# A fifth room between scores and weighting, warming steps and a new written-out order in a pre-norm attention and expert kernel

## Chip, core and metric

One core of one Trainium2 chip runs the whole kernel. The metric is the device time of one execution in microseconds (us); the kernel before has a median of 277.43 us over three runs (276.83 to 277.89).

## What is computed

The input is `x`, four batches of 1024 tokens with 128 features. One layer is applied: attention, then a mixture of experts, each on a layer-normed input and each with a residual.

```python
x = x + attn(layernorm(x));  x = x + moe(layernorm(x))
# attn, 8 heads of 16
Q, K, V = silu(x@Wq), silu(x@Wk), silu(x@Wv);  U = x@Wu
s = (Q @ K.T + rel_bias[i - j + 255]) / 4      # set to NEG above the diagonal
w = silu(s)                                    # and for keys that are all zero
out = (w @ V) * silu(U)
# moe: top 2 of 8 gates, softmax over the two
y = sum_e gate[e] * ((x @ w_in[e].T) @ w_out[e].T)
```

The weights are `silu`, not a softmax, so that no row sum is needed. An expert has no nonlinearity between its two matrices; the kernel folds them into one matrix of 128 x 128 (`wfold`).

## The kernel before

**Groups.** The queries are worked on in groups of 512 (four tiles of 128), two per batch; the last group is split into two of 256, which makes nine. For a group, the keys are gone through in 73 units over the whole kernel. One unit fills four score banks of up to 512 columns: keys against queries for the four heads 2k + parity, k = 0 to 3.

**Score step (S, `attend`).** TensorE (PE) fills four PSUM banks with scores (L492). Near the diagonal VectorE (DVE) adds the bias from the table `near` and writes the sum to a room `w` in SBUF (L511), and ScalarE (ACT) applies silu in place (L514). Far from it the bias is one number for a head, and ACT goes from PSUM to `w` alone (L519). **Weighting step (W, `weigh`).** PE multiplies `w` with V and adds it up in one bank `av` (L470); after a group's last unit DVE gates the sum (L479). The rooms `w` come from the pool `wpool`, which has `WBUFS = 4` of them: a score step whose room is still unread has to wait for the weighting step four units back.

**The other steps.** P and Q prepare the first and the second half of a batch: norm, K, Q, V, U. The key mask takes a DVE comparison `nz` (L387), a small product, and `kmask` (L394). K makes the bias tables (`constants`) and clears the second of the two rooms for V (L257, GpSimd, POOL). G folds experts. C, D and E (`finish`) carry a group from attention to its gates; the norm's statistics and the gates take a round trip through DRAM on the SyncE (SP) queue. X, Y and Z apply the experts, a tile at a time: `experts` scales the input by each gate first and sums in PSUM (L96, L650); `experts_then_gates`, for the last two groups, takes the product with all experts first and gates afterwards, in a scratch tile `both` from `spool` (L672 to L685). The result leaves by `store` (L691).

**What sets the order.** Each engine executes its instructions in the order in which they are written. The string `ORDER` is that order: `load_all` comes first, and then each letter advances its lane to its next `yield`. PSUM has a ring of seven banks for everything but `av` (`RING`, handed out in turn by `misc()`); a step that asks for a bank waits until the instruction that reads the bank's last use is done. The 73 letters S are 0 to 4 ahead of the 73 letters W.

**The start.** `load_all` begins with `HEAT = 18` dummy products of 128 x 128 on PE (`ident` against itself, L96; each is four 32-row pieces and two passes). POOL clears the first room for V in one memset of 2048 columns (L169) and some small tiles. DVE widens the bias row, `rb` (L146), and only then normalizes the first block (L316, L321, L330, with POOL's power L325); PE transposes it (L337) and ACT copies it to `xnT` (L338).

Of the kernel before, what the change touches and what calls it, by code (L numbers as in the profile page):

```python
# [8 lines left out]
F32 = mybir.dt.float32  # L9
# [7 lines left out]
P = 128  # L17
H = 8
HD = 16
NQ = 4  # L20
# [3 lines left out]
SB = 512  # L24
TPB = SB // P
# [6 lines left out]
OFF = -3.0e38  # L32
EULER = 2.718281828459045
RING = 7
HEAT = 18
LAST = 2


# [2 lines left out]


ORDER = (
    "PPQPQKPPQKPKSPSPSQQSWWSWGSWQPWSQWSPSCSWQPSCCQKWGSPWPSWWSWPKQSWGSWSWSCWSWPSWPSGDSQQDPQWSCPP"
    "WWSWQWSQDWSSCESCDWPEPCSCWQWEDCSWPCSWCQDSWDCSWDDDCPGSPPWQCDSQWSWSGWESGWPSWSWSDEWECQEDPEDEEC"
    "GDQWWSXSWSQCXECSCEXSECQWSCEXPWPWSDEDQPCQWSDDWDSYDSWQEESWDCYCCYCDCSWWWESCYCSPCWCCSZDCQWSEDZ"
    "SDEWPEQQWSEZSDWWDQDCDQSDCDWZDSDCXCSEWEWEWCCESWEECXXEESQWDSEWDDXSEDEYCSEDDWWDSCCYDCCCSCDCDY"
    "CSCYCDWCDESDWWEDDSZDWWEDWDEYEEYEYYZECZEEECEYEECZXEYEXEEZCZZZXZXZ"
)


# [1 line left out]
def preln_silu_attention_moe(  # L53
# [14 lines left out]
    nc = tc.nc  # L68
    B, S, D = x.shape
    NR = rel_biasT.shape[1]  # L70
    NT = S // P
    NB = S // SB
    NC = HID // P
    WBUFS = 4

    cpool = ctx.enter_context(tc.tile_pool(name="cpool", bufs=1))
    xpool = ctx.enter_context(tc.tile_pool(name="xpool", bufs=B))
# [10 lines left out]
    def misc():  # L88

        return ps_s.tile([P, SB], F32, tag="bank", name="bank")  # L90

    def product(out, stationary, moving, start=True, stop=True):


        for q in range(0, P, 32):
            nc.tensor.matmul(  # L96
                out[q : q + 32, :], stationary[:, q : q + 32], moving, start=start, stop=stop
            )
# [13 lines left out]
    NPAD = MAXLEN - 1 + TAB  # L112
    FAR = TAB - MAXLEN

    rb = spool.tile([P, 8 * D], F32, tag="both", name="rb")[:H, :NPAD]
    wcat = cpool.tile([P, 4, D], F32, tag="wcat", name="wcat")
    wgT = cpool.tile([P, GW], F32, tag="wgT", name="wgT")
    stats_d = dpool.tile([2 * B * NB, 32, 4, 32], F32, tag="stats_d", name="stats_d")
# [8 lines left out]
    def load_near(par, to, src, pitch, n):  # L127
# [2 lines left out]
            bass.AP(src.tensor, src.offset, [[1, P], [2 * pitch, NQ], [1, n]]),  # L130
        )

    def load_all():

        pt = misc()
        for i in range(HEAT):
            product(pt[:, :P], ident, ident)

        load_x(0, 0)
        nc.scalar.dma_start(rb[:, NPAD - NR :], rel_biasT)  # L140
        load_w(1, wk)
        load_near(0, FAR, rel_biasT, NR, MAXLEN)

        nc.vector.memset(one, 1.0)
        nc.scalar.activation(one, one, AF.Silu)
        nc.vector.tensor_copy(  # L146
            rb[:, : NPAD - NR], rb[:, NPAD - NR : NPAD - NR + 1].to_broadcast([H, NPAD - NR])
        )
        nc.scalar.dma_start(ext[:, :], rb)
        load_w(0, wq)  # L150
        load_x(0, 1)
        load_near(1, FAR, rel_biasT[1:2, :], NR, MAXLEN)

        load_near(0, FAR - P, ext[0:1, FAR - P :], NPAD, P)
        load_near(1, FAR - P, ext[1:2, FAR - P :], NPAD, P)
        load_w(2, wv)
        load_w(3, wu)
        nc.gpsimd.memset(wgT, 0.0)

        nc.gpsimd.memset(ones8, 1.0)  # L160
        nc.gpsimd.affine_select(
            out=ones8, in_=ones8, compare_op=ALU.is_ge, fill=0.0,
            base=0, pattern=[[-HD, H]], channel_multiplier=1,
        )
        nc.gpsimd.affine_select(
            out=ones8, in_=ones8, compare_op=ALU.is_ge, fill=0.0,
            base=HD - 1, pattern=[[HD, H]], channel_multiplier=-1,
        )
        nc.gpsimd.memset(vps[0], 0.0)  # L169
        nc.gpsimd.memset(euler, EULER)  # L170
        for st in stats:
            nc.gpsimd.memset(st, 0.0)
        nc.scalar.dma_start(wgT[:, :E], w_gateT)

        for n in range(2, B * NB):
            load_x(n // NB, n % NB)
        for e0 in range(0, E, 2):

            if e0 % 4 == 0:
                room = gpool.tile([P, 2, 2, 2, NC, D], F32, tag="wide", name=f"w_in_out_{e0}")  # L180
            both = room[:, e0 // 2 % 2]
            for t, w in zip((both[:, 0], both[:, 1]), (w_in, w_outT)):
                nc.sync.dma_start(t, w[e0 : e0 + 2].rearrange("e (c p) d -> p e c d", p=P))
            experts_in.append(both)
# [18 lines left out]


    one = cpool.tile([P, 1], F32, tag="one", name="one")
    ident = cpool.tile([P, P], F32, tag="ident", name="ident")
    make_identity(nc, ident)
    mhalf = cpool.tile([P, TPB], F32, tag="mhalf", name="mhalf")
# [18 lines left out]
    def constants():  # L227


        pt = misc()  # L230
        nc.tensor.matmul(
            pt[:, :H], rb[:, :1].to_broadcast([H, P]), ident[:H, :H], start=True, stop=True
        )
        for par in range(2):
            nc.scalar.copy(
                near[:, par, :, : FAR - P],
                pt[:, :H].rearrange("p (k q) -> p q k", q=2)[:, par, :]
                .unsqueeze(2).to_broadcast([P, NQ, FAR - P]),
            )
        nc.vector.tensor_scalar(cscaled, pt[:, :H], SCALE, None, ALU.mult)  # L240
        yield

        for par in range(2):
            diag = near[:, par, :, TAB - P : TAB]
            nc.gpsimd.affine_select(
                out=diag, in_=diag, compare_op=ALU.is_ge, fill=NEG,
                base=P - 1, pattern=[[0, NQ], [-1, P]], channel_multiplier=-1,
            )
            nc.vector.tensor_copy(near[:, par, :, TAB:], diag)  # L249
            yield  # L250

        nc.gpsimd.iota(
            rank, pattern=[[0, TPB], [-1, E]], base=E, channel_multiplier=0,
            allow_small_or_imprecise_dtypes=True,
        )
        yield
        nc.gpsimd.memset(vps[1], 0.0)  # L257
        yield

    def fold():  # L260

        for e0, both in zip(range(0, E, 2), experts_in):
            for e in range(2):
                pt = misc()
                for c in range(NC):
                    product(
                        pt[:, :D], both[:, 0, e, c, :], both[:, 1, e, c, :],
                        start=(c == 0), stop=(c == NC - 1),
                    )
                nc.scalar.copy(wfold[:, e0 + e, :], pt[:, :D])  # L270
                yield
# [368 lines left out]
    def experts(b, t0, gated):  # L640

        y = xs[b][:, t0 : t0 + TPB, :]
        for i in range(TPB):
            pt = misc()
            for e in range(E):
                product(
                    pt[:, :D], gated[:, i, e, :], wfold[:, e, :],
                    start=(e == 0), stop=(e == E - 1),
                )
            nc.vector.tensor_tensor(y[:, i, :], pt[:, :D], y[:, i, :], ALU.add)  # L650
            if i == TPB - 1:
                store(b, t0, TPB, y)
            yield

    def experts_then_gates(b, t0, nt, x2T, gates):

        EH = SB // D
        y = xs[b][:, t0 : t0 + nt, :]
        for i in range(nt):

            both = spool.tile([P, 2 * EH, D], F32, tag="both", name="both")
            gy, other = both[:, : EH + 1, :], both[:, EH + 1 :, :]
            for e0 in (EH, 0):
                pt = misc()
                product(
                    pt, x2T[:, i, :], wfold[:, e0 : e0 + EH, :].rearrange("p e d -> p (e d)")
                )
                for e in range(EH):
                    ye = pt[:, e * D : (e + 1) * D]
                    gate = gates[:, i, e0 + e : e0 + e + 1]  # L670
                    if e0:
                        nc.scalar.activation(  # L672
                            other[:, e, :] if e < EH - 1 else gy[:, EH, :], ye, AF.Copy, scale=gate
                        )
                    else:
                        nc.vector.scalar_tensor_tensor(
                            gy[:, e, :], ye, gate,
                            other[:, e, :] if e < EH - 1 else y[:, i, :],
                            ALU.mult, ALU.add,
                        )  # L680
                yield
            half = EH // 2
            nc.vector.tensor_tensor(gy[:, :half, :], gy[:, :half, :], gy[:, half:EH, :], ALU.add)
            nc.vector.tensor_tensor(gy[:, 0, :], gy[:, 0, :], gy[:, EH, :], ALU.add)
            nc.vector.tensor_tensor(y[:, i, :], gy[:, 0, :], gy[:, 1, :], ALU.add)  # L685
            if i == nt - 1:
                store(b, t0, nt, y)
            yield

    def store(b, t0, nt, y):  # L690
        nc.sync.dma_start(  # L691
            out[b, t0 * P : (t0 + nt) * P, :].rearrange("(i p) d -> p i d", p=P), y[:, :nt, :]
        )
# [9 lines left out]
    lanes["P"] = [prepare(b, 0) for b in range(B)]  # L703
    lanes["Q"] = [prepare(b, 1) for b in range(B)]
    lanes["G"] = [fold()]
    lanes["K"] = [constants()]

    def step(lane):
# [52 lines left out]
```

## Time and profile before

| what | us |
|---|---|
| median of the runs (lowest, highest) | 277.43 (276.83, 277.89) |
| the profiled execution | 276.35 |
| its span, from first to last instruction | 274.6 |
| PE, from its first score step to the start of its last product | 13.2 to 270.1 |
| last arithmetic (DVE L685) ends | 271.8 |
| DVE busy, 0 to 110 us | 80.3 |
| DVE busy, 110 us to the end | 149.5 |
| mean cost of one `w` add on DVE, 512 columns (L511) | 0.68 |

The page gives busy time by engine, then the span in slices, the chain of work that ended last, and the costliest groups of instructions. PE's busy time is not a measure of its load: the ends of matmuls are modelled, so an engine that waits inside a row of matmuls can still be shown as busy. What PE loses is read from the starts of its matmuls: equal rows of matmuls have equal start-to-start times where nothing holds them.

### The profile page before, as it was taken

What the parts mean: (1) busy time and instruction counts of PE and PEld (TensorE: products, weight loads), DVE (VectorE), ACT (ScalarE), POOL (GpSimd) and SP (SyncE); (2) the same over time, 40 slices, a digit from 0 to 9 for tenths busy, and PEclk for the clock granted to TensorE, in tenths of its full rate; (3) what the DMA queues carried; (4) which work ended last, traced back from release to release, by engine and by line L of the source; (5) the groups of instructions that cost most, each with busy time, mean ns of one, the idle gap of its engine ahead of it and who ended that gap; (6) DMA issues with size and microseconds to landing.
All of it is one profiled execution on the core that took longest, in us unless ns stands there. A gap on an engine that the chain in (4) does not pass through costs nothing.

```text
span 274.6 us, 10777 instructions
## 1 busy us (share of the span) xinstructions
PE 264.8 (96%) x4694; PEld 145.2 (53%) x4694; DVE 229.8 (84%) x594; ACT 194.0 (71%) x316; POOL 88.6 (32%) x101
## 2 busy tenths in 40 slices
PE   7799999999999999999999999999998999999993
PEld 7344443344444234444465347565675776775872
DVE  5597656569976977999989898999899998898994
ACT  2568998879899898889768866575965467684030
POOL 7410136600544712372024241351360343111010
PEclk9999999999999999999999999999999999999999
DMA  5899930330004032272080483217022621845022
GB/s 176 214 301 287 290 128 5 117 117 2 0 5 124 35 77 84 81 300 91 5 309 2 123 333 97 79 41 284 31 82 97 256 80 43 308 143 211 5 60 60
DMA packets 33315, 34.88 MB, mean 127 GB/s; under 512 B 4068, under 2 KB 29676, under 8 KB 32372
## 3 DMA queue, kind: packets, MB, share of 16 engines
q1 hardware_dynamic: 32516, 33.89, 38.3%
q8 instruction: 37, 0.61, 0.9%
q10 hardware_dynamic: 752, 0.31, 0.4%
q14 instruction: 10, 0.08, 0.1%
HBM read 31.74 MB, written 2.45 MB: 124 GB/s over the span
## 4 chain that ended last, share of the span: by engine, by line
PE 85%; DVE 8%; POOL 2%; issue 2%; ACT 1%; POOLq 0%; DVEq 0%
PE bank L96 31%; PE bank L492 29%; PE av L470 22%; DVE w L511 3%; DVE gated L635 2%; PE bank L541 2%; POOL rstd L325 1%; PE bank L569 1%; POOL vp L169 1%; DVE den L608 1%; ACT w L519 1%; DVE attended L479 0%; ACT w L514 0%; POOL xn L330 0%; DVE near L249 0%
## 5 line engine op out<-in xcount | busy, mean ns | idle before, releaser
L511 DVE TENSOR_TENSOR w<-bank,near 128x512 f32<-128x512 f32 (+2 forms) x220 | 116.5, 589 | 18.0 <-PE bank L492 15.0
L514 ACT ACTIVATE w<-w 128x1024 f32<-128x1024 f32 (+2 forms) x110 | 98.2, 915 | 40.5 <-DVE w L511 37.8
L492 PE MATMUL bank<-qT,kT 32*128 32x512 f32 (+3 forms) x864 | 91.0, 483 | 1.4 <-DVE x L650 0.8
L519 ACT ACTIVATE w<-bank,cscaled 128x512 f32<-128x512 f32 (+3 forms) x136 | 70.2, 604 | 10.4 <-PE bank L492 5.9
L470 PE MATMUL av<-w,vp 128*32 128x512 f32 (+3 forms) x864 | 74.0, 454 | 0.4 <-DVE turned L276 0.3
L492 PEld LDWEIGHTS bank<-qT,kT 32*128 32x128 f32 x864 | 39.7, 184 | 39.5 <-DVE w L511 14.9
L96 PE MATMUL bank<-wfold,gated 128*32 128x128 f32 x1792 | 53.9, 273 | 0.3 <-issue 0.3
L96 PEld LDWEIGHTS bank<-wfold,gated 128*32 128x32 f32 x1792 | 48.3, 110 | 9.2 <-issue 4.6
L470 PEld LDWEIGHTS av<-w,vp 128*32 128x32 f32 x864 | 23.2, 109 | 34.6 <-issue 26.3
L635 DVE TENSOR_TENSOR gated<-gated,x2T 128x1024 f32<-128x1024 f32 x28 | 35.8, 1288 | 0.9 <-DMA gated<-gates_d 0.9
L289 POOL TENSOR_TENSOR stats<-rs,mhalf 128x4 f32<-128x4 f32 x13 | 13.2, 1019 | 46.8 <-DVE rs L288 44.0
L96 PE MATMUL bank<-xnT,wcat 128*32 128x512 f32 x192 | 24.3, 597 | 0.5 <-ACT xnT L338 0.4
L605 POOL TENSOR_TENSOR ex<-euler,d 128x4 f32<-128x4 f32 (+1 forms) x9 | 9.6, 1061 | 41.0 <-DVE d L603 37.0
L406 POOL TENSOR_TENSOR vp<-v,kmask 128x256 f32<-128x256 f32 x16 | 9.8, 632 | 31.8 <-ACT v L404 31.8
L305 POOL TENSOR_TENSOR mean<-attended,mean 128x512 f32<-128x512 f32 x7 | 9.3, 1324 | 19.8 <-DMA mean<-stats_d 19.8
L672 ACT ACTIVATE both<-bank,gates 128x128 f32<-128x128 f32 x16 | 4.5, 375 | 14.9 <-DVE gates L619 11.0
L305 POOL TENSOR_TENSOR mean<-xT,mean 128x512 f32<-128x512 f32 x6 | 7.7, 1283 | 20.4 <-DMA mean<-stats_d 20.4
L96 PEld LDWEIGHTS bank<-xnT,wcat 128*32 128x32 f32 x192 | 5.3, 109 | 13.3 <-issue 5.2
L371 ACT ACTIVATE kT<-bank,sel 128x512 f32<-128x512 f32 x16 | 11.0, 690 | 0.2 <-PE bank L96 0.2
L306 POOL TENSOR_TENSOR x2T<-mean,x2T 128x512 f32<-128x512 f32 x7 | 9.8, 1402 | 0.6
L284 DVE BATCH_NORM_STATS2 stats<-x 128x6 f32<-128x256 f32 x26 | 9.8, 418 | 0.1
L96 PEld LDWEIGHTS bank<-w_in_out 128*32 128x32 f32 x256 | 7.0, 110 | 4.5 <-DVE w L511 2.4
(87 smaller groups left out, 204.4 us busy)
## 6 DMA issues: line engine op xcount, KB each, us to landing
gated<-gates_d SPq DMA_DIRECT2D x7, 2048.0 KB, 8.2
mean<-stats_d SPq DMA_DIRECT2D x13, 256.0 KB, 3.6
x<-in_L_attn_x SPq DMA_DIRECT2D x8, 256.0 KB, 6.4
w_in_out<-in_L_ffn_w_in SPq DMA_DIRECT2D x4, 512.0 KB, 7.4
w_in_out<-in_L_ffn_w_out SPq DMA_DIRECT2D x4, 512.0 KB, 7.5
xT<-in_L_attn_x_T SPq DMA_DIRECT2D x8, 256.0 KB, 4.4
x2T<-stats_d SPq DMA_DIRECT2D x7, 256.0 KB, 3.7
out<-x SPq DMA_DIRECT2D x7, 256.0 KB, 2.3
```

Of the source, the lines that this page charges most:

```text
L96: nc.tensor.matmul(out[q : q + 32, :], stationary[:, q : q + 32], moving, start=start, stop=stop)
L284: nc.vector.bn_stats(st[:, 3 * i : 3 * i + 6], src[:, i : i + 2, :].rearrange("p i d -> p d i"))
L289: nc.gpsimd.tensor_tensor(st[:, TPB * 3 : TPB * 4], rs, mhalf, ALU.pow)
L305: nc.gpsimd.tensor_tensor(mean, srcT, mean, ALU.subtract)
L306: nc.gpsimd.tensor_tensor(dst, mean, dst, ALU.mult)
L371: nc.scalar.activation(kT[:, par, s0 : s0 + SB], pk, AF.Silu, scale=sel[:, par : par + 1])
L470: nc.tensor.matmul(acc[k * 32 : (k + 1) * 32, nt * P - n : nt * P], vp[:, j, par, k, :, :].rearrange("p q c -> p (q c)"), w[:, k, c : c + ...
L492: nc.tensor.matmul(ps[k][:, c : c + n], kT[k * 32 : (k + 1) * 32, par, j * P : (j + 1) * P], qT[k * 32 : (k + 1) * 32, lo : lo + n], start ...
L511: nc.vector.tensor_tensor(w[:, k, :nn], ps[k][:, :nn], near_of(k, parts), ALU.add)
L514: nc.scalar.activation(w[:, k : k + 2, :nn], w[:, k : k + 2, :nn], AF.Silu, scale=SCALE)
L519: nc.scalar.activation(w[:, k, lo:hi], ps[k][:, lo:hi], AF.Silu, bias=cscaled[:, h : h + 1], scale=SCALE,)
L635: nc.vector.tensor_tensor(wide_g[:, i], wide_g[:, i], x2T[:, i : i + 1, :].to_broadcast([P, E, P]), ALU.mult)
```

## The change

Seven edits, and no arithmetic of the result is changed.

- `WBUFS` goes from 4 to 5. The tile `both` of the last experts, and the start's `rb`, no longer have a room of their own in `spool`; they take their turn in the ring of rooms `w`.
- `HEAT` goes from 18 to 10, and the dummy products use a tile `heat` that DVE sets to 1, in place of POOL's `ident`.
- A lane H (`warm`) does two dummy products per step; the order has six H: three before the first score step, one in the middle, two at the very end.
- Each room for V is cleared in four memsets of 512 columns.
- `experts` stores two tiles at a time in place of four, `experts_then_gates` one in place of two.
- The order string is new. The same steps stand in it, with S up to 5 ahead of W. The first bias step K stands ahead of the first transpose, K's other steps are spread, and the four last X (experts of the third-last group) are mixed with the last Z so that the string ends in X, then HH. In the string before it ends in XZ.

```diff
-HEAT = 18
+HEAT = 10
-    "PPQPQKPPQKPKSPSPSQQSWWSWGSWQPWSQWSPSCSWQPSCCQKWGSPWPSWWSWPKQSWGSWSWSCWSWPSWPSGDSQQDPQWSCPP"
...
-    "CSCYCDWCDESDWWEDDSZDWWEDWDEYEEYEYYZECZEEECEYEECZXEYEXEEZCZZZXZXZ"
+    "PPQKHPHPQPQHPKSPSQQKPSWWSGSKWGSPKWQPWSQWSSWPSQPPSWWCSWPSWQSSCWSPPPQSQWSWSWWPSWPSQQWSWWSDGC"
...
+    "WEYCEDDDWSWESCWDCDCWDYCWDEWDDDZEEYYEYZEYEEEYEYEZECECECEZEZCZXZZXZXZXHH"
-    WBUFS = 4
+    WBUFS = 5
-    rb = spool.tile([P, 8 * D], F32, tag="both", name="rb")[:H, :NPAD]
+    rb = wpool.tile([P, NQ * SB], F32, tag="w", name="rb")[:H, :NPAD]
+    def clear(vp):
+        for i in range(0, NT, 2):
+            nc.gpsimd.memset(vp[:, i : i + 2], 0.0)
-            product(pt[:, :P], ident, ident)
+            product(pt[:, :P], heat, heat)
-        nc.gpsimd.memset(vps[0], 0.0)
+        clear(vps[0])
+    heat = cpool.tile([P, P], F32, tag="heat", name="heat")
+    nc.vector.memset(heat, 1.0)
-        nc.gpsimd.memset(vps[1], 0.0)
+        clear(vps[1])
+    def warm():
+        while True:
+            pt = misc()
+            for i in range(2):
+                product(pt[:, :P], heat, heat)
+            yield
-            if i == TPB - 1:
-                store(b, t0, TPB, y)
+            if i % 2:
+                store(b, t0 + i - 1, 2, y[:, i - 1 :])
-            both = spool.tile([P, 2 * EH, D], F32, tag="both", name="both")
-            gy, other = both[:, : EH + 1, :], both[:, EH + 1 :, :]
+            both = wpool.tile([P, NQ * TPB, D], F32, tag="w", name="both")
+            gy, other = both[:, : EH + 1, :], both[:, EH + 1 : 2 * EH, :]
-            if i == nt - 1:
-                store(b, t0, nt, y)
+            store(b, t0 + i, 1, y[:, i:])
+    lanes["H"] = [warm()]
```

More of the change, by code (lines that the diff above doesn't have):

```diff
@@ L34 @@
 RING = 7
-HEAT = 18
+HEAT = 10
 LAST = 2
 ORDER = (
-    "PPQPQKPPQKPKSPSPSQQSWWSWGSWQPWSQWSPSCSWQPSCCQKWGSPWPSWWSWPKQSWGSWSWSCWSWPSWPSGDSQQDPQWSCPP"
-    "WWSWQWSQDWSSCESCDWPEPCSCWQWEDCSWPCSWCQDSWDCSWDDDCPGSPPWQCDSQWSWSGWESGWPSWSWSDEWECQEDPEDEEC"
-    "GDQWWSXSWSQCXECSCEXSECQWSCEXPWPWSDEDQPCQWSDDWDSYDSWQEESWDCYCCYCDCSWWWESCYCSPCWCCSZDCQWSEDZ"
-    "SDEWPEQQWSEZSDWWDQDCDQSDCDWZDSDCXCSEWEWEWCCESWEECXXEESQWDSEWDDXSEDEYCSEDDWWDSCCYDCCCSCDCDY"
-    "CSCYCDWCDESDWWEDDSZDWWEDWDEYEEYEYYZECZEEECEYEECZXEYEXEEZCZZZXZXZ"
+    "PPQKHPHPQPQHPKSPSQQKPSWWSGSKWGSPKWQPWSQWSSWPSQPPSWWCSWPSWQSSCWSPPPQSQWSWSWWPSWPSQQWSWWSDGC"
+    "WSWQPPDSQDWSSCESWWSDWCGECQDSWPSWCHSWCCQDCESCDWDDSCDQGCDWECPPSWSCWWESWSGQWSGWSGEQQPSDWPWSWQ"
+    "DDEDECQWSQCCXSWECPSEXCESCWSQPCDDWQPSDEWXSXESWPDWEECSDCCCYWCCSCCYDSWDCSCWDYCSWEYSWCEZQSWSWE"
+    "DEQQZPEESPZWEWQDDSCDWDDSWDCZSDCDDWEDSXCEEQQECCSECWXEEXESEDDXWSWEDWECESYCCWDCSWCCSYDDCDSWSD"
+    "WEYCEDDDWSWESCWDCDCWDYCWDEWDDDZEEYYEYZEYEEEYEYEZECECECEZEZCZXZZXZXZXHH"
 )
```

## The prediction

> **What bounds the kernel now.** I read the busy times and the chain of the page first, then the waits, then the timeline at three places: the start, a hole in a score step, the end.
>
> ```profile
> PE 264.8 (96%) x4694; PEld 145.2 (53%) x4694; DVE 229.8 (84%) x594; ACT 194.0 (71%) x316; POOL 88.6 (32%) x101
> ...
> PE 85%; DVE 8%; POOL 2%; issue 2%; ACT 1%; POOLq 0%; DVEq 0%
> ```
>
> PE carries 85% of the chain. Its 96% says little, since ends are modelled, so I took from the trace the start-to-start times of PE's matmuls by row: a unit's four 512-column scores take 1.07 us undisturbed, their weighting 0.86, one expert tile (64 matmuls) 1.77. At these paces PE's work from the first score step (13.2 us) to 270.1 is 237.5 us. What rows took over their own kind's undisturbed pace (lower quartile, after equal predecessors, holes over 0.06 us) adds up to **14.3 us of waiting**: 9.05 in score steps, 2.82 in weighting steps, 2.4 elsewhere. The rest, 5, is the price of changing kinds of step, which the new order leaves alone (66 changes from scores to 32-column products against 66).
>
> ```profile
> PEld bank L492 <- DVE w L511: 14.9, 25, 0.8
> PEld bank L492 <- ACT w L519: 5.8, 11, 0.8
> PEld av L470 <- ACT w L514: 2.7, 6, 0.8
> ```
>
> The columns are us in total, times, longest. They are waits of the weight load, partly covered by matmuls still running, so their sum isn't PE's loss; but they name the releasers. Score steps wait for banks that DVE or ACT still reads, and weighting steps for silu. A hole as an example:
>
> ```profile
> 57.84 0.50 PE L492 MATMUL bank<-qT,kT 32*128 32x128 f32 x6
> 58.79 1.13 PE L492 MATMUL bank<-qT,kT 32*128 32x128 f32 x10 [0.45 <-ACT w L519]
> ```
>
> Six of sixteen score matmuls go, then the bank ring is full for nearly 1 us. DVE is the second bound: 80.3 of the first 110 us are busy, but 149.5 of the remaining 162 to its last result, 92%.
>
> **The fifth room and the order.** I summed every step's PE work at the paces above. In the old string a weighting step is written a median of 6.45 us of PE work after the end of its score step (tenth percentile 3.9, least 2.8); in the new 8.41 (4.8, 3.8). What must happen between is, for a unit near the diagonal, four adds (2.48 us, DVE L511) and the second silu (1.06, L514), 3.5 us, and whatever DVE has queued before. So the 2.82 us of weighting waits have 1 to 2 us more cover each, more than the longest release of 0.8 in the row above: I take 2.0 away (ends 0 and 2.82). Score waits are not about rooms: DVE and ACT still read the seven banks, and there are still seven. The room helps them only by letting PE do a weighting step, 0.86 us, in the meantime if the order puts one there. Bounds: all of 9.05 goes, or waits grow (the slower rival). A change of order that leaves DVE's work the same must lie near the bottom: I take 1.0. The middle gives **-3.0**. DVE's idle share after 110 us (12 us) leaves room for that. The adds need no room sooner than before: none of DVE's listed waits in L511 is for a weighting step, so rooms delay PE, not DVE.
>
> **The H in the middle** and its bank: 16 matmuls by 27.7 ns (an expert tile's 1.77 us over 64), **+0.44**; 0 if it falls in a hole, 0.44 if not. The pair HH at the end is 0.9 us of PE beside a store, which takes longer: 0.
>
> **The start.**
>
> ```profile
> 1.80 1.80 POOL L169 MEMSET vp<- 128x2048 f32 x1
> ...
> 2.48 1.58 DVE L146 COPY rb<-rb 8x256 f32<-8x256 f32 x1 [1.57 <-DMA rb<-in_L_attn_rel_bias]
> ...
> 3.99 0.74 DVE L316 BATCH_NORM_STATS2 st<-x 128x6 f32<-128x256 f32 x2
> ...
> 5.02 1.02 POOL L325 TENSOR_TENSOR rstd<-rs,mhalf 128x4 f32<-128x4 f32 x1 [1.10 <-DVE rs L321]
> ...
> 7.39 0.66 PE L337 MATMUL bank<-ident,xn 128*128 128x128 f32 x4
> ```
>
> A copy of 256 columns lasts 1.58 us because it finishes 0.45 us after POOL's memset, 3.61. [...] The transposes at 7.39 also wait for the old heating, which runs to 7.46; the xn they need was ready at 7.02. [...] The copy of `near` ahead of `nz` (DVE L249, 11.45 to 12.29) goes behind it, but `nz` started at 12.28 with the key at 12.24, so that alone gives 0.04, and the second copy (0.42) now stands among the adds. K's two ACT copies of `near` (0.54 each) come ahead of xnT on ACT, behind DMA issues that end about 5.9, so they end at 7.0, just in time. Sum: between -0.9 and +0.4, I take **-0.5**.
>
> [...] In this trace the dummy matmuls go every 53.4 ns until 5.3 us and every 27.3 afterwards, and the record of the granted clock begins at 5.27, 3.8 us after the first. [...]
>
> **The end.**
>
> ```profile
> 270.41 0.29 DVE L650 TENSOR_TENSOR x<-bank,x 128x128 f32<-128x128 f32 x1 [0.52 <-PE bank L96]
> 270.62 0.41 DVE L683 TENSOR_TENSOR both<-both 128x256 f32<-128x256 f32 x1
> ...
> 271.47 0.29 DVE L685 TENSOR_TENSOR x<-both 128x128 f32<-128x128 f32 x1
> ```
>
> After the last product (L650's bank) three more adds of the gated path stand ahead of the last store; PE's products are already over. In the new string the last Z is ahead of the last X, so the end is one add of 0.29: the last store is issued at 270.7 instead of 271.8, **-1.05**. Store to landing was 1.86 (271.79 to 273.65, 128 KB, with 256 KB more ahead of it); the new last one is 128 KB with 64 ahead: 0 to 0.3 less, taken as 0.
>
> **Stores.** 18 instead of 9, each some 0.39 us of SP (the last two issues). SP is in order and a store waits for its add, so loads of the norm's statistics behind it wait as well. Those loads wait for a later DVE transpose in any case, and the whole queue is some 90 issues by 0.4, 36 of 275 us: 0, up to +3.5 if all nine further issues were on the path. **The scratch tile in the ring**: a Y or Z step needs the room of five allocations before, whose weighting is long past; 0. **Clearing the second V room** in pieces: POOL is idle two thirds of the time, 0.
>
> **Sum.** -3.0 + 0.44 - 0.5 - 1.05 = -4.1. The span goes from 274.6 to 270.5, the profiled execution from 276.35 to 272.25; the median of the runs is 1.08 above the latter, so 277.43 becomes **273.3**.
>
> **Rivals.**
> - *Nothing in the middle* (DVE is full): the 2 us that weighting no longer waits turn into score waits. For it: DVE at 92% after 110 us, and its work is the same 235 us in either string. Against: it idles 12 us there. -1.1: **276.3**.
> - *The queue pays in full*: more work in hand means half of the 14.3 goes, -7.1, -8.2 in all: **269.2**. For it: 14.3 is there to be had, and the lead over weighting is 3.8 units on average after 3.0. Against: seven banks.
> - *Slower, by bunching*: the new string uses its longer lead to set DVE work closer. Between 158 and 196 us of PE work it asks 41.0 us of DVE for 38.1 of PE; the old one 39.9 for 39.8 in the like stretch. Summing for stretches of 36 steps the busiest engine's work, DVE scaled to its union, gives 250.6 against 247.9, 2.7 more. If that is waited out and no wait saved, -1.1 + 2.7 = +1.6: **279.0**. It decides once fewer than 1.6 us of waits are saved elsewhere.
>
> **How the numbers follow.** Forecast 0.56, nothing in the middle 0.17, full pay 0.17, bunching 0.10. A measurement of this kernel tells about 0.5%, 1.4 us, from no change. The forecast spreads by about 2.5 either way from the start's and the middle's bounds, so nearly all of it and of full pay is faster, and a part of the second: faster 0.78, same 0.12, slower 0.10. The range, 268.9 to 277.2, leaves out bunching and the lower half of full pay.
>
> **What would show it.** The copy of rb near 0.5 to 0.7 us long; first score matmul at 12.5 to 13; waits of `av` L470 for L514 below 1 us in total; score waits for L511 hardly less; the last DVE result 0.3 after the last expert product. A first score step after 13.3, or DVE waiting as before while PE's score waits grow beyond 10 us, would make the prediction wrong.

## The result, and the profile after

The changed kernel takes **284.39 us** (median of four runs, 283.61 to 286.21), against 277.13 for the kernel before, run beside it. The ratio is 1.0271 [1.0213, 1.0329]: it is slower by 7.3 us, where 273.3 was forecast. The profiled execution is the longest of the four, 286.21 us with a span of 284.4. Slow executions, over 1.5% above the fastest of their kernel (one of e4's four, one of e7's ten, two of e10's ten), are left out of the medians below.

The page of the changed kernel, its busy times and the shares of the chain that ended last:

```profile
PE 268.4 (94%) x4726; PEld 145.0 (51%) x4726; DVE 234.1 (82%) x595; ACT 193.9 (68%) x316; POOL 95.1 (33%) x107
...
PE 56%; DVE 22%; DMA 7%; issue 5%; ACT 4%; SPq 2%; POOL 2%; POOLq 0%; ACTq 0%; DVEq 0%
```

PE's share of the chain fell from 85% to 56%, DVE's rose from 8% to 22%. The steps are the same but for the warming, yet DVE is busy 4.3 us longer (229.8 before), 3.5 of it in the experts' scalings (L650), and POOL 6.5 (88.6 before): some instructions last longer. And the engines wait for each other. The waits of the changed kernel (us in total, times, longest; PEld is PE's weight load); L507 is the score line, L485 the weighting, L526 the adds and L534 and L529 the two silu, which were L492, L470, L511, L519 and L514:

```profile
DVE w L526 <- PE bank L507: 22.2, 23, 5.0
...
PEld bank L507 <- DVE w L526: 9.9, 17, 0.8
...
PEld bank L507 <- ACT w L534: 9.1, 15, 1.0
...
PE bank L96 <- POOL xnT L321: 2.6, 1, 2.6
...
PEld av L485 <- ACT w L529: 2.4, 4, 0.8
...
PE bank L96 <- ACT w L534: 2.1, 1, 2.1
```

The first row is new to the argument. Its like before the change is:

```profile
DVE w L511 <- PE bank L492: 15.0, 17, 2.3
```

DVE waits 22.2 us for scores instead of 15.0. At the score line, PE's weight loads wait less for DVE (9.9 after 14.9) and longer for ACT (9.1 after 5.8). Counted by the prediction's method, PE waits 23.1 us instead of 14.3: 11.96 in score steps (9.05 before), 3.61 in weighting steps (2.82), 5.3 in the 512-column projections and 2.2 elsewhere (2.4 for these two before). So 5.1 of the 8.8 more lie outside scores and weighting, and nearly all of that is two waits of a projection, the two rows for `PE bank L96`.

To see where, I gave every step of the string its place in the trace and took PE's work written up to there (at the prediction's paces) from the time of its first matmul. What remains is time lost. Places at which both strings have done the same steps, but for a letter or two, make stretches that can be compared:

| lost, in us, per stretch (ends in the changed kernel's time) | 0-25 | 25-58 | 58-122 | 122-213 | 213-246 | 246-276 | sum |
|---|---|---|---|---|---|---|---|
| before | 7.5 | 2.6 | 6.6 | 5.7 | 1.9 | 1.2 | 25.5 |
| the change | 8.3 | 6.7 | 4.5 | 7.9 | 6.8 | 1.1 | 35.3 |
| all edits, old string (e1) | 9.7 | 2.7 | 6.7 | 5.9 | 1.7 | 1.3 | 28.0 |

(The old string without warming steps has 1.8 us less work on PE, which is why e1 is no slower than before.) Two stretches stand out, 25 to 58 and 213 to 246 us. The places below hold the largest single losses in them, and one between them.

**At 40 us**, in the timeline of the changed kernel (start, length, engine, line; in brackets the idle time before it and its releaser):

```profile
40.10 1.06 PE L96 MATMUL bank<-xnT,wcat 128*32 128x512 f32 x8
40.54 1.27 POOL L320 TENSOR_TENSOR mean<-xT,mean 128x512 f32<-128x512 f32 x1 [2.89 <-DMA mean<-stats_d]
42.45 1.26 POOL L321 TENSOR_TENSOR xnT<-mean,xnT 128x512 f32<-128x512 f32 x1 [0.65 <-DMA xnT<-stats_d]
43.77 1.92 PE L96 MATMUL bank<-xnT,wcat 128*32 128x512 f32 x16 [2.61 <-POOL xnT L321]
```

The second batch's projections (letters 46 and 47, PP) are written straight behind a first one; their normed input comes back from DRAM and POOL only at 43.7. PE starts nothing else in the 2.61 us between: its next matmul is theirs, at 43.77. In the kernel before, POOL's second product starts nearly as late (41.7 us against 42.45), and the like projection stands at 44.5 us with no wait.

**At 139 us**, the same view:

```profile
139.25 4.51 DVE L650 TENSOR_TENSOR gated<-gated,x2T 128x1024 f32<-128x1024 f32 x2
140.54 2.14 POOL L321 TENSOR_TENSOR xnT<-mean,xnT 128x512 f32<-128x512 f32 x1
144.02 1.13 PE L507 MATMUL bank<-qT,kT 32*128 32x512 f32 x4 [0.65 <-DVE x L665]
```

Two of the experts' scalings, 1.22 us each when alone, last 4.51 together beside POOL's product, itself 2.14 instead of 1.28. A score step needs the bank of the add that is queued behind them.

**At 214 us** stands the second-largest single loss:

```profile
210.42 1.27 POOL L320 TENSOR_TENSOR mean<-attended,mean 128x512 f32<-128x512 f32 x1
210.47 1.24 DVE L623 TENSOR_SCALAR den<-ex 128x4 f32<-128x4 f32 x1 [0.71 <-POOL ex L620]
...
211.76 1.28 POOL L321 TENSOR_TENSOR x2T<-mean,x2T 128x512 f32<-128x512 f32 x1
211.84 2.29 DVE L650 TENSOR_TENSOR gated<-gated,x2T 128x1024 f32<-128x1024 f32 x1
...
216.04 0.70 ACT L534 ACTIVATE w<-bank,cscaled 128x128 f32<-128x128 f32 x2 [3.61 <-DVE w L526]
...
216.46 1.07 PE L96 MATMUL bank<-xnT,wcat 128*32 128x512 f32 x8 [2.07 <-ACT w L534]
```

Two DVE instructions that each start just behind a POOL product last 1.24 and 2.29 us (0.16 and 1.22 elsewhere). DVE's adds come later for it, ACT waits 3.61 us for them, and a projection that needs the bank ACT reads waits 2.07.

**At 225 us**:

```profile
224.16 0.92 PE L507 MATMUL bank<-qT,kT 32*128 32x128 f32 x11
226.35 0.70 PE L507 MATMUL bank<-qT,kT 32*128 32x256 f32 x5 [1.28 <-issue]
```

A score step stops after 11 of 16 matmuls, and the profile shows nothing that it waited for.

**The start.**

```profile
1.80 1.92 POOL L136 MEMSET vp<- 128x512 f32 x4
2.45 1.74 DVE L151 COPY rb<-rb 8x256 f32<-8x256 f32 x1 [1.40 <-DMA rb<-in_L_attn_rel_bias]
...
13.34 1.14 PE L507 MATMUL bank<-qT,kT 32*128 32x512 f32 x8
```

The copy is longer, not shorter (1.74 against 1.58), and ends 0.47 after the last of the four memsets, as it ended 0.45 after the one. The first score step comes at 13.34 (13.21 before).

**The end.**

```profile
279.58 0.41 DVE L698 TENSOR_TENSOR both<-both 128x256 f32<-128x256 f32 x1
...
280.10 0.29 DVE L699 TENSOR_TENSOR both<-both 128x128 f32<-128x128 f32 x1
280.43 0.29 DVE L700 TENSOR_TENSOR x<-both 128x128 f32<-128x128 f32 x1
280.64 0.28 DVE L665 TENSOR_TENSOR x<-bank,x 128x128 f32<-128x128 f32 x1
280.75 1.14 SPq L705 DMA_DIRECT2D out<-x  x2
```

The last X is last in the string, but the gated path's three adds still stand ahead of its add on DVE. From the start of PE's last product (the warming apart) to DVE's last result it is 1.02 us instead of 1.69; from there to the end of the span 3.49 instead of 2.87, since a store of the tile before is issued just ahead.

### The profile page after: what moved, and what is told of

It is laid out like the page before. It is cut to its first block, busy times and chain, and to the rows that moved or that the text cites. A ratio compares the mean times of both kernels' runs of the same rounds, so it can differ in the third digit from the quotient of the medians.

```text
span 284.4 us, 10866 instructions
## 1 busy us (share of the span) xinstructions
PE 268.4 (94%) x4726; PEld 145.0 (51%) x4726; DVE 234.1 (82%) x595; ACT 193.9 (68%) x316; POOL 95.1 (33%) x107
## 4 chain that ended last, share of the span: by engine, by line
PE 56%; DVE 22%; DMA 7%; issue 5%; ACT 4%; SPq 2%; POOL 2%; POOLq 0%; ACTq 0%; DVEq 0%
PE bank L96 21%; PE bank L507 19%; PE av L485 15%; DVE w L526 9%; DVE gated L650 5%; DMA w_in_out<-in_L_ffn_w_out 3%; ACT w L534 3%; DMA ext<-rb 2%; DMA xnT<-stats_d 2%; SPq L105 2%; ACT w L529 1%; PE bank L556 1%; DVE stats L299 1%; DVE x L665 1%; POOL ex L620 1%
## 5 line engine op out<-in xcount | busy, mean ns | idle before, releaser
L526 DVE TENSOR_TENSOR w<-bank,near 128x512 f32<-128x512 f32 (+2 forms) x220 | 116.1, 588 | 24.5 <-PE bank L507 22.2
L529 ACT ACTIVATE w<-w 128x1024 f32<-128x1024 f32 (+2 forms) x110 | 98.3, 923 | 43.5 <-DVE w L526 40.9
L507 PE MATMUL bank<-qT,kT 32*128 32x512 f32 (+3 forms) x864 | 92.1, 483 | 3.1 <-issue 1.3
L534 ACT ACTIVATE w<-bank,cscaled 128x512 f32<-128x512 f32 (+3 forms) x136 | 70.1, 611 | 13.6 <-PE bank L507 9.5
L485 PE MATMUL av<-w,vp 128*32 128x512 f32 (+3 forms) x864 | 74.4, 455 | 0.0
L507 PEld LDWEIGHTS bank<-qT,kT 32*128 32x128 f32 x864 | 39.8, 183 | 44.0 <-issue 12.6
L96 PEld LDWEIGHTS bank<-wfold,gated 128*32 128x32 f32 x1792 | 49.1, 110 | 12.1 <-issue 6.4
L96 PE MATMUL bank<-wfold,gated 128*32 128x128 f32 x1792 | 53.7, 273 | 0.0
L485 PEld LDWEIGHTS av<-w,vp 128*32 128x32 f32 x864 | 22.2, 109 | 34.8 <-issue 27.2
L650 DVE TENSOR_TENSOR gated<-gated,x2T 128x1024 f32<-128x1024 f32 x28 | 39.3, 1412 | 0.0
L304 POOL TENSOR_TENSOR stats<-rs,mhalf 128x4 f32<-128x4 f32 x13 | 14.6, 1122 | 52.6 <-DVE rs L303 44.8
L96 PE MATMUL bank<-xnT,wcat 128*32 128x512 f32 x192 | 24.0, 597 | 5.3 <-POOL xnT L321 2.6
L620 POOL TENSOR_TENSOR ex<-euler,d 128x4 f32<-128x4 f32 (+1 forms) x9 | 12.2, 1355 | 47.2 <-DVE d L618 47.2
L96 PEld LDWEIGHTS bank<-xnT,wcat 128*32 128x32 f32 x192 | 4.9, 109 | 16.3 <-issue 4.6
L321 POOL TENSOR_TENSOR x2T<-mean,x2T 128x512 f32<-128x512 f32 x7 | 11.3, 1615 | 0.5
L96 PE MATMUL bank<-w_in_out 128*32 128x128 f32 x256 | 8.6, 275 | 1.0 <-DMA w_in_out<-in_L_ffn_w_out 1.0
```

The lines of the kernel that those rows point to most:

```text
L96: nc.tensor.matmul(out[q : q + 32, :], stationary[:, q : q + 32], moving, start=start, stop=stop)
L304: nc.gpsimd.tensor_tensor(st[:, TPB * 3 : TPB * 4], rs, mhalf, ALU.pow)
L321: nc.gpsimd.tensor_tensor(dst, mean, dst, ALU.mult)
L485: nc.tensor.matmul(acc[k * 32 : (k + 1) * 32, nt * P - n : nt * P], vp[:, j, par, k, :, :].rearrange("p q c -> p (q c)"), w[:, k, c : c + ...
L507: nc.tensor.matmul(ps[k][:, c : c + n], kT[k * 32 : (k + 1) * 32, par, j * P : (j + 1) * P], qT[k * 32 : (k + 1) * 32, lo : lo + n], start ...
L526: nc.vector.tensor_tensor(w[:, k, :nn], ps[k][:, :nn], near_of(k, parts), ALU.add)
```

## The experiments

Theory A1: the string costs the time, because it puts DVE's work closer together (the prediction's rival) and steps ahead of their inputs. Rivals: one of the other edits does (ring, memsets, stores), or the fifth room lets writes go earlier and so makes collisions. `NEW` and `OLD` are the two strings; "the change" is the kernel with all edits.

**e1: everything but the string.** `ORDER = OLD`.

> All edits but the order string, which is the one of before (no H then). Theory A (the string costs it all, by two places: a projection at 41 us that is written ahead of its norm, and from 158 us of PE work on a bunching of DVE work that meets POOL's norm multiplies): 276 to 278, at the time of before, since the start gained nothing. Rival B (the other edits cost: the fifth room and what moved into the ring, pieces, twice the stores, less heating): 281 to 284.

277.48 us, ratio 1.0015 [0.9985, 1.0045]. The 7.3 us are the string's; the other edits together show neither gain nor loss, within an interval that reaches 1.2 us.

**e2: the string with four rooms.** `WBUFS = 4`.

> The changed kernel with four rooms in place of five; the new string stays, with scores up to 5 ahead, so the fifth unit's adds and silus wait for the first unit's weighting. Theory A: not faster than the changed kernel; 285 to 290, since the string was written for five. Rival B (the fifth room or the ring's use costs): at or under 281.

296.56 us, 1.0706 [1.0632, 1.078]. The string needs its fifth room: without it 12.2 us more than the change.

**e11: the old string with four rooms.** e1 and `WBUFS = 4`.

> All edits but two: the old string, and four buffers between scores and weighting. Theory 1 (a fifth buffer is only good for what the string does with it, and the old string never has five score steps ahead): 277.5 us, as with five buffers and the old string (277.5). Theory 2 (the fifth buffer lets ScalarE's and DVE's writes of weights go earlier under any string, and another edit costs as much): 279 us or more.

276.57 us, 1.0001 [0.9971, 1.0031]. A fifth room is worth nothing where the string has no fifth score step ahead, and it harms nothing.

**e3 and e4: one half of the string each.** `ORDER = NEW[:162] + "P" + OLD[158:]` less one E; `ORDER = OLD[:158] + "E" + NEW[162:]` less one P.

> The changed kernel with the new string up to its letter 162 (121 us, PE work 102) and the old string from the matching place on (one P moved ahead and one E dropped at the seam). Theory A: the loss of the first part alone, by the ledger of PE work against time 2.7 at the seam (19.3 against 16.6): 279 to 281. If only the second half matters: 277. If the lead carried over the seam matters: above 283.

> The changed kernel with the old string up to its letter 158 and the new one from the matching place on (one E put in, one P dropped at the seam). Theory A: the loss of the second part, 7.3 less the first part's 2.7, some 4 to 5, in profile the same growth between 158 and 212 us of PE work: 281 to 283. If the first part matters alone: 277.

280.56 us, 1.0105 [1.0033, 1.0177]: the first half costs 3.4 (3.1 against e1). The second half gave 286.51, 1.0346 [1.0262, 1.043], but at its seam, where the two orders don't fit, PE waits 3.71 us for a norm, and behind that the granted clock is halved from 121.8 to 128.7 us, so its size can't be used.

**e5: the projections at 40 us four letters later.** `ORDER = NEW[:46] + NEW[48:52] + "PP" + NEW[52:]`.

> The changed kernel with one edit of its string: the two steps P of the second batch at 43.8 us (its keys and queries) go behind the next S, W, W and C. Theory A (they stand ahead of their norm's second DMA, and PE waits 2.8 us): 281.5 to 282.5, with no wait for POOL's xnT at 40 to 44 us. If the wait only moves to the next step that needs the second batch: 284.

282.46 us, 1.0232 [1.016, 1.0305]: 1.9 us less by the medians; the interval overlaps the change's. The timeline of this kernel at the same place:

```profile
41.87 1.27 POOL L321 TENSOR_TENSOR xnT<-mean,xnT 128x512 f32<-128x512 f32 x1 [0.37 <-DMA xnT<-stats_d]
...
45.57 0.64 PE L96 MATMUL bank<-xnT,wcat 128*32 128x512 f32 x4
```

The projection starts 2.4 us after its input is there, and isn't waiting for it. The saving stays: in the trace the loss is 1.7 us lower right behind this place, 2.1 at 164 us and 3.4 at the end, as some of POOL's products now fall elsewhere.

**e6 and e7: no reads by POOL beside DVE.** In the change, and in the kernel before, the three two-input products of the norm on POOL are left out, with memsets of about the same length in their place (1.52 us for three, against 1.28); the norm isn't computed.

```diff
-            nc.gpsimd.tensor_tensor(add, add, srcT, ALU.add)
+            for _ in range(3):
+                nc.gpsimd.memset(add[:, :448], 0.0)
...
-        nc.gpsimd.tensor_tensor(mean, srcT, mean, ALU.subtract)
-        nc.gpsimd.tensor_tensor(dst, mean, dst, ALU.mult)
+        for t in (mean, dst):
+            for _ in range(3):
+                nc.gpsimd.memset(t[:, :448], 0.0)
```

> The changed kernel with POOL's three multiplies and adds of every column-wise norm left out, and three memsets of 448 columns in place of each, which write for about as long but read nothing; the outputs are not the layer's. Theory A1 (in the second half DVE's gating multiplies, both inputs in SBUF, collide with POOL's reads, and the new string sets them side by side): the changed kernel gains 4 to 6, to 278 to 280, and the gap to the same edit of the kernel before shrinks from 7 to about 3. Rival A2 (bunching alone; the collisions are incidental): both gain alike, and the gap stays at 6 to 7.

> The kernel before with the same POOL instructions left out and replaced by memsets. Theory A1: DVE's excess over its own medians is 6.3 us in the kernel before against 10.3 in the changed one, and half of it at most is on the path: 275 to 276.5. Rival A2: the same gain as the changed kernel has from this edit.

281.61 us, 1.0196 [1.0119, 1.0274], and 275.29, 0.994 [0.9904, 0.9976]: 2.8 us less with the new string, 1.8 with the old. The group of the scalings (total, mean ns), first in the change, then in e6:

```profile
L650 DVE TENSOR_TENSOR gated<-gated,x2T 128x1024 f32<-128x1024 f32 x28 | 39.3, 1412 | 0.0
```

```profile
L652 DVE TENSOR_TENSOR gated<-gated,x2T 128x1024 f32<-128x1024 f32 x28 | 33.6, 1210 | 0.0
```

Before the change it was 35.8. So the collisions are real, 5.7 us of DVE in the new string and 2.2 in the old, and in e6 the losses at 139, 188 and 214 us are gone from the trace: the projection that waited 2.07 us now follows at 210.4 with no wait.

What this is worth in time is not settled. By the medians the gap between the strings only falls from 7.3 to 6.3 (and is 7.9 with e16 below in place of e7), which speaks against the collisions as the main cause. But e6's four executions are 278.82, 280.70, 282.52 and 282.93 us at mean granted clocks of 1.0, 0.994, 0.988 and 0.988, so its median holds the clock as well. In the profiled executions, all four at full clock, the products are worth 7.4 us in the change (spans of 284.4 and 277.0) and 1.4 before (274.6 and 273.2). Each of these is one execution, the change's is its longest and e6's its shortest, so 7.4 is rather too much.

**e8: the old string with its last four letters turned.** e1 with `ZXZX` at the end in place of `XZXZ`.

> All edits, the old string, but for its last four letters: ZXZX in place of XZXZ, so that the last product is followed by one add. The prediction's step for the end, -1.05, then shows against the old string with all edits (277.5): 276.3 to 276.7. If the last product ends later since PE is a step behind there: 277.5.

277.42 us, 1.0035 [1.0002, 1.0069]. Having X last gives nothing, by itself and in the kernel before's order.

**e9, e10 and e12: the stretch from 211 us on.** `NEW[:309] + "Q" + OLD[306:]`; `OLD[:306] + NEW[309:]` less one Q; e9 with e5's repair.

> All edits of the change, the new order string up to its letter 309 and the old one from its letter 306 (with one Q to make the counts agree): only the stretch from about 211 us on is old again. Theory 1 (the loss of the new string sits in several places, each where DVE's work is bunched or PE is put ahead of its input, and some 4 us of it lie between 211 and 227 us): 280 to 281 us. Theory 2 (the loss is made before 211 us; what is late after that would be late under any string): 284 us, no better than the change.

> The reverse: the old string up to its letter 306, the new one from letter 309 on, all other edits as in the change. Theory 1: 277.5 plus about 4, 281 to 282 us. Theory 2: 277.5 us, as with the old string throughout.

> The change with two repairs of its string at once: the two projections of letters 46 and 47 stand four letters later, and the string is the old one from its letter 306 on. Theory 1 (the places are separate and their losses add): 1.9 us from the first and 3.5 to 4.5 from the second, 278.5 to 279.5 us. Theory 2 (a wait removed is taken up again at the next place): 281 to 282 us.

285.89 us, 1.0318 [1.0263, 1.0373]; 278.86, 1.0074 [1.0038, 1.0111]; 284.94, 1.0277 [1.0226, 1.0327]. e9 and e12 fit neither theory: in e9 the seam has two holes of its own (1.8 and 2.3 us, at 213 and 216), so they say little of the letters. e10, between its two forecasts, says more: the new letters from 309 on cost 1.4 us behind old ones, while the stretch from 213 to 246 us loses 5.1 more in the change than in e1. Most of that is thus owed to what stands ahead of it. e9 shows something else. Busy times by stretch in e9 (stretch, its length, PE, PEld, DVE, ACT, POOL, then the granted clock):

```profile
205.00:215.00 10.00, 8.40 (x224) 6.28 (x221) 8.97 (x19) 5.43 (x9) 4.47 (x3) 1.00 0.14 45
215.00:230.00 15.00, 12.89 (x240) 8.48 (x244) 9.51 (x32) 4.46 (x8) 3.48 (x5) 0.77 0.40 145
```

PE waits here for V and for DVE, and its granted clock is halved from 217.25 to 224.07 us, a mean of 0.77 over the 15 us: rows of weighting with 256 columns then take 0.43 us instead of 0.22. By estimate from these figures, 6.83 us at half the clock are 3.4 us of PE's work. So the halved clock costs 3.4 by this estimate, beside the two holes' 4.1; that the holes brought it about is not shown.

The clock is also a rival for the whole. Behind the wait at 40 us it is halved for 3.41 us in e3, e9 and e13 (from 45.4, 43.2 and 43.9 us), and not in the profiled executions of the change and of e6, which wait there too. The other three executions of the change have a mean clock of 0.993 to 0.994, as one such stretch would make it (estimate: half of 3.41 in 282 us is 0.006). But the one at full clock is the longest of the four, so the 7.3 us do not need it.

**e13: the warming steps moved.** The hole at 225 us stands behind PE's matmul number 3409, in the change, in e5 and in e6, whatever the time. The DMA view of the change says what comes at that place, first from 217 to 223 us (DMA's busy tenths in 40 slices; a queue's packets, MB and share; an issue):

```profile
DMA  0000003999402009950995099829995599579957
...
gated<-gates_d SPq DMA_DIRECT2D x1, 2048.0 KB
```

and then from 223.9 to 224.9:

```profile
q8 instruction: 1, 0.02, 5.8%
```

Queue q8, which the profile names instruction, moves 37 pieces of 16 KB in this run, and there are 4726 matmuls with their weight loads, so one for each 128 matmuls on average (before, 37 for 4694); that the pieces are PE's program is the author's estimate from this count, and no run tests it. Elsewhere they come 68 to 169 matmuls apart; this one comes 236 after the one ahead of it, when the 2 MB of gates have gone (218.2 to 224.1), and ends at 224.9. PE goes on 1.46 later. e13 moves two of the six H behind the last letter (`NEW` without its third and fourth H, then `HH`), so that each later matmul's number is lower by 32.

> The change with two of its six warming steps (the third of the start and the one in the middle) moved behind the last letter, so that every later matmul has a number lower by 32 in PE's program. Theory C (the hole of 1.65 us at 225 us is the load of the next piece of PE's program, held up behind the 2 MB load of gates): the piece is then needed two score units' halves later, after the load, and the hole goes: 1.3 to 1.6 us, with 0.44 for the step in the middle and 0 to 0.5 at the start, 282 to 282.6 us. Theory D (the hole belongs to the score step, a bank or a room that isn't shown): it stays, and the two steps give 0.4 to 0.9, 283.5 to 284 us.

283.65 us, 1.0245 [1.0197, 1.0293]. The timeline of e13:

```profile
223.20 0.94 PE L507 MATMUL bank<-qT,kT 32*128 32x128 f32 x16
224.07 1.06 PE L96 MATMUL bank<-wfold,gated 128*32 128x128 f32 x27
225.54 1.18 PE L96 MATMUL bank<-wfold,gated 128*32 128x128 f32 x35 [0.41 <-issue]
```

The score step now runs through, and the hole, 0.69 from start to start instead of 1.65, is in the experts' products behind it: again behind matmul 3409, and again 1.42 after the piece's end. By the place theory C holds: the hole keeps to the matmul's number and not to the score step. That the gates' load holds the piece up is not shown, for in other such loads a piece came through in the middle (at 122.5, 239.8 and 262.1 in the change). The time is where theory D had it: 0.7 us, of which 0.44 is the middle H that went, so 0.3, within what the runs scatter. The old string has the same hole 512 matmuls on, behind number 3921, of 0.58 to 1.10 us (before, e1, e8): it is only in part the new string's.

**e14, e15, e16: both repairs; the same without POOL's products; the old string without them.**

> The warming steps moved as in the kernel before this one, and the two projections at 40 us four letters later (which alone gave 1.9 us). If the places are separate: 280 to 281 us. If what is saved at 40 us is taken up again later: 282 us or more.

> The two repairs, and in the norm GpSimd's three products of two inputs (sum with the input, minus mean, times deviation) are left out and memsets of about the same length stand in their place, so that the norm isn't computed. If the projections at 40 us, the load of the program and the collisions of DVE with GpSimd are all that the string costs: within 1 us of the old string with the same left out, 276 to 277 us. If there is a further cause: 278.5 us or more.

> All edits but the string, and the same three GpSimd products left out as in the kernel before this one (the norm isn't computed). It is the measure for that kernel. The kernel before the change with the same left out took 275.3 us, and all edits with the old string cost nothing: 275.3 to 275.8 us.

282.17 us, 1.017 [1.0113, 1.0227]; 277.53, 1.003 [1.0007, 1.0053]; 273.74, 0.9888 [0.9835, 0.994]. e14 is hardly below e5. Leaving the products out gives 4.6 us here and 3.7 with the old string. e15 and e16 stay 3.8 us apart, so there is a further cause: the three named ones are not all. The size is less sure, for e7, the other measure of the old string without the products, is 275.29: 2.2 from e15.

**e17 and e18: only the first 60 us old.** `OLD[:59] + "S" + NEW[62:]` less one C, warming steps last; the same without POOL's products of the norm, which isn't computed.

> All edits of the change; the string is the old one up to its letter 59 (about 53 us), then one S, and the new string from its letter 62 on less one C (so that the counts agree), with all warming steps in the rest behind the last letter. If the first 60 us cost the 3 to 4 us that the traces suggest: 280 to 281 us. If the loss is in the rest: 283 us or more.

> The same, with GpSimd's three products of the norm left out (the norm isn't computed). If what is left over sits in the first 60 us: 274 to 275 us, as with the old string throughout (273.7). If it is spread over the rest: 276.5 us or more.

281.35 us, 1.0157 [1.0124, 1.0191], and 278.12, 1.0052 [1.0017, 1.0087]. The old order of the first 60 us gives back 3.0 of the 7.3, the 1.9 of e5 and the moved warming steps among them. Most of the remainder is not there: e18 stands 4.4 us above e16. About 1.0 of this is lost at e18's start, where the clock is on record only from 13.49 us (first score step at 14.62 us, 13.63 in e16, in their profiles).

## Why the prediction was wrong

**The failing step is "The fifth room and the order", -3.0.** It took the distance in PE work from a score step to its weighting step (6.45 us to 8.41) for cover, and concluded that the waits of weighting fall from 2.82 by 2.0 and those of scores by 1.0. They rose, to 3.61 and 11.96, and its sign, `av` waiting for L514 less than 1 us in all, came out at 2.4 after 2.7. The larger part of the growth, 5.1 of 8.8, fell in the waits "elsewhere", 2.4 before, for which the sum has no term. Two things were wrong with it. It measured one chain of several: a projection behind its norm's round trip was put closer, and PE waits 2.61 us there (1.9 in time, e5). And it took PE's work as the measure while DVE and ACT hand out the banks: a step written later is no help if PE stands at a bank meanwhile, and with units closer together PE stood there more, and DVE in turn waited longer for the next scores (15.0 to 22.2 us; 15.1 in e1). This second part is read from the waits; no run tests it alone. A third cost had no term either: DVE's scalings beside POOL's products last 3.5 us longer in total than before (39.3 against 35.8), and the projection at 214 us waits 2.07 for it (not in e6). The room as such did what was said of it, nothing by itself (e11) and much for the string written for it (e2).

**The rivals.** Bunching was on the right side with 279.0; it was mis-sized, since its 2.7 was a sum of loads and the waits were 8.8 more by the prediction's measure. I gave it 0.10 for want of a reason why a new order should lose. That it sets DVE's work closer was counted before, and was the sign. That this is the mechanism for the whole is not shown: see below.

**The start, -0.5: 0.** No run shows this gain, or a copy of `rb` of 0.5 to 0.7 us. Beside four memsets the copy lasted 1.74 us, beside the one 1.58, and it ended 0.47 after the last of them, as it ended 0.45 after the one. The first score step came 0.13 later (13.34 after 13.21), not 0.5 sooner. Less heating was free in the change: the record of the granted clock begins at 4.53 us there and at 5.27 before. Whether the three H made it free is not shown: in kernels with ten products and the old beginning, which has no H, the clock was halved again from 9.2, 9.1 and 8.3 us for 3.41 us (e4, e16, e17), and it was not in e1, e8, e10 and e11.

**The end, -1.05: 0.** The string ends as read, but the adds of the gated path are queued ahead of the last one on DVE, so 0.67 was won, and 0.62 lost in the store behind another (e8: nothing).

**Stores, the ring for `both`, the second V room, 0: right** (e1 has them all, 1.0015). **The H in the middle, +0.44**, was not tried alone; e13 has room for it.

**The account of the 7.3 us**, from medians: 1.9 the projection at 40 us (e5); 0.7 the hole behind matmul 3409 and the middle H (e13); about 1 more from DVE beside POOL than the old string has (2.8 and 4.6 against 1.8 and 3.7); 3.8 not assigned (e15 against e16). The first three were each shown to exist in the trace; the sizes of the second and third are within the scatter. The profiled executions give the third up to 6 (7.4 against 1.4, at e6) and leave only 1.9 between e15 and e16; but e16's is the longest of its four (275.59, its clock halved from 9.08 to 12.49 us), so 1.9 is rather too little. So how the 7.3 divides between the collisions and the remainder stays open. The remainder lies for the most part behind the first 60 us (e18). Bunching would fit it, for both engines wait on each other there, but no run spread DVE's work while leaving all else.

## What to carry to other kernels

When a hand-written order changes, measure every chain that ends in the engine it is written for, not only the one that the change is about: for each step take the distance to the latest of its inputs, a round trip through DRAM included (here 2.61 us of waiting at 40 us). The fifth room was worth what the order did with it (12.2 us with the new string, e2; nothing with the old one, e11), so price the order, and price it with the engine that hands out the banks. Moving a step to be last in the string need not move it last in another engine's queue: here three adds on DVE stayed ahead of the last one. And compare executions at the same granted clock: a halved clock followed PE's wait at 40 us in three of these runs (for 3.41 us in e3, e9 and e13), and a median then holds both.

## What the runs showed of the hardware

- Queue q8, named instruction in the profile, moved 37 pieces of 16 KB in the change and 37 before, for 4726 and 4694 matmuls with their weight loads; that they are PE's program is the author's estimate. Behind the 2 MB load of gates in the change (218.2 to 224.1 us) a piece came 236 matmuls after the one before, and PE stopped at a fixed matmul number (3409, with the old string 3921) until 1.27 to 1.47 us after a piece's landing (before, the change, e1, e5 to e8, e11, e13, e15, e16). The profile calls it "issue".
- A scaling of two inputs on DVE, 1.22 us in the median, took 1.72 to 2.29 beside a POOL product (six of the 28 in the change), and the POOL product up to 2.32 instead of 1.28. In e6, where memsets stand in the place of POOL's products of the norm, the 28 have a mean of 1.210.
- With POOL's memset cut into four, DVE's copy beside it was no shorter (1.74 us against 1.58) and ended 0.47 us after the last piece (0.45 after the one).
- The granted clock is on record from 3.43 us after the first of ten dummy products in the change and from 3.76 after the first of 18 before (at 4.53 and 5.27 us); over the other runs it is 2.69 (e15) to 12.39 (e18).
- In mid-kernel the granted clock was halved for 3.41 us (e3, e9, e12, e13, e14) or 6.83 (e4, e9) at a time, and PE's rows then took twice as long (0.43 us instead of 0.22 in e9). PE's wait at 40 us (2.6 us by the starts of its matmuls in e9 and e13, 3.5 in e3) was followed by it, and the same wait in the change (2.8) and e6 (2.6) was not.
